# A Restormer block on one core: layer-norm statistics of two interleaved tiles per instruction, the TensorE convolution in two of three units of every band, and one common set of PSUM banks

## The chip, the cores and the metric

The kernel runs on one core of one Trainium2 chip. The metric is the device time of one execution in microseconds, given as the median of three runs. One execution was recorded by the hardware profiler; its page and its trace are what the prediction argues from. The engines are called by the names that the profile uses: PE (TensorE, matrix multiplication), PEld (its weight loads), DVE (VectorE), ACT (ScalarE), POOL (GpSimd) and SP (SyncE, which here only issues transfers).

## What is computed

The input is 16 images of 128 channels by 96 by 96 pixels in float32. For each image the reference computes a transformer block whose attention runs over channels, and then a feed-forward part with a depthwise convolution:

```
xn1 = layernorm(x over channels)
q, k, v = xn1 @ wq.T, xn1 @ wk.T, xn1 @ wv.T        # 8 heads of 16 channels
attn = softmax(l2norm(q) @ l2norm(k).T * scale)     # 16 x 16 per head, sums over all pixels
x = x + (attn @ v) @ wp.T
xn2 = layernorm(x over channels)
h1 = w_in @ xn2                                     # 128 -> 512 channels, 1x1
h2 = depthwise 3x3 of h1                            # 512 channels, zero padding
x = x + w_out @ gelu(h2)                            # 512 -> 128 channels, 1x1
```

## The kernel before, in words

Channels lie on the 128 partitions. An image is cut into 24 units of 4 rows (384 pixels, three tiles of 128 pixels) and 8 bands of 12 rows (three units each); the 512 hidden channels are four chunks of 128.

**Layer norms** (`norm_batch`, line 349). The norm runs over channels, which are partitions, so each tile is turned by PE into PSUM (`forth`, L374; pixels are now on partitions), DVE takes its statistics (`stats`, one `bn_stats` per tile, L380), five short DVE operations on 128x6 make mean and variance of the six tiles of a batch (`moments`, L389 to L393), POOL raises the variance to the power -0.5 (`power`, L397), one more short DVE operation makes the shift (`shift`, L401), ACT scales the tiles out of PSUM (`scaled`, L408), PE turns them back (`back`, L417), and ACT places them in the padded image `xn` (`place`, L432 for the second norm, L436 for the first). A `bn_stats` writes six numbers: count, mean and sum of squared deviations of the elements at even positions, and the same of those at odd positions; `moments` merges the two halves. The first norm (names with `a`) also adds each tile's product with itself to a 128x128 Gram matrix on PE (`gram`, L424), from which `attention` makes a single 128x128 matrix per image; the second norm (names with `b`) begins with `mix` (L364, that matrix times `xn`) and `residual` (L368, on DVE).

**Convolution.** For each band and each chunk, `conv_job` makes 14 rows of hidden values on PE in three matmuls of 490, 490 and 392 columns (`hidden`, L599), ACT copies each from PSUM into `h1` (`kept`, L606), and the nine taps of the depthwise filter are shared out. ACT multiplies tap 0 straight into `h3`, and taps 1 and 2 into buffers `pr` (L615). POOL issues a transfer that adds one `pr` to the other and a second that adds the sum to `h3` (`by_dma`, L626). The other six are DVE instructions on 128x1152 that each add to the same `h3` (`tap`, L623); these are called taps below. ACT then applies the gelu (L646). For chunk 3 of five of the eight bands (`PE_BANDS`, bands 1, 3, 5, 6 and 7) there is no such job: `by_matmuls` (L660) makes the convolved values of each unit by nine accumulating matmuls with a combined filter, and ACT takes the gelu out of PSUM (L668). `ffn_out` (L684) multiplies the four chunks by `w_out`, unit by unit; DVE adds the result to the image (L691), and SP stores the band.

**PSUM.** There are eight banks of 512 floats per partition: three for turned tiles (`p_tr`), one for tiles turned back (`p_b`), two shared by hidden rows, mixes and the PE convolution (`p_h`), one for the output (`p_o`), one for the Gram matrix (`p_g`).

**The order of the work.** `Plan` keeps a list of operations with an engine, a duration, a place (its priority, counted in convolution jobs) and the tiles that it reads and writes. `Plan.order` plays them through with these durations: an engine that falls idle takes the operation of lowest place among those that are ready and whose buffers are free. The order found is written out as the program, and each engine then runs its own part of it strictly in turn. An operation behind another of the same engine counts as ready when that one's duration is over; behind another engine's, after its `result` time, which is 430 to 550 ns longer for PE, DVE and ACT. Pools in `IN_TURN` give out their buffers in the order of the places. There are nine `h3` tiles (each one chunk of a band), three `h1` and three `pr`.

Of the kernel before, what the change touches and what calls it, by code (L numbers as in the profile page):

```python
# [20 lines left out]
PE_BANDS = (1, 3, 5, 6, 7)  # L21
DMA_TAPS = (1, 2)
BU = 2
# [3 lines left out]
IN_TURN = ("h3", "h1", "pr", "xb", "x1")  # L27
IN_ORDER = ("PE", "DVE", "ACT")
# [4 lines left out]
class Plan:  # L33
# [7 lines left out]
    def __init__(self, **pools):  # L41
        self.free = dict(pools)
        self.ops, self.writer, self.readers, self.users = [], {}, {}, {}

    def op(self, engine, ns, place, work, reads=(), writes=(), result=None):
# [21 lines left out]
        self.ops.append((engine, ns, place, work, list(needs), new, ns if result is None else result))  # L67

    def order(self):
# [27 lines left out]
        def room(k):  # L97
# [5 lines left out]
            for p, n in need.items():  # L103
                if free[p] < n:
# [3 lines left out]
        def dispatch(engine, time):  # L108
# [13 lines left out]
            for t in o[5]:  # L122
                free[t[0]] -= 1
# [16 lines left out]
        while events:  # L140
            time, _, kind, what = heapq.heappop(events)
            if kind != "look":
                for f in followers[what]:
                    if (ops[f][0] == ops[what][0] in IN_ORDER) == (kind == "idle"):
# [4 lines left out]
            if kind == "done":  # L149
                for t in held[what]:  # L150
                    pending[t] -= 1
                    if not pending[t]:
                        free[t[0]] += 1
                        wake(t[0], time)
                continue
# [11 lines left out]
def tile_restormer_block(  # L167
# [30 lines left out]
    TPU = UT // P  # L198
    NTOK = H * W
    HP, WP = H + 2, W + 2  # L200
    D = C // HEADS
    assert C == P and UT % P == 0 and H % BR == 0 and NCH == 4
# [22 lines left out]
    mhalf = const.tile([P, BU * TPU], F32, name="mhalf")  # L225
# [22 lines left out]
    with tc.tile_pool(name="setup", bufs=1) as sp, tc.tile_pool(name="setup2", bufs=2) as sp2:  # L248
# [10 lines left out]
        def transposed(dst, src):  # L259
            pt = p_tr.tile([P, P], F32, tag="tr", name="pt")  # L260
# [7 lines left out]
        pc = p_tr.tile([1, 2 * P], F32, tag="tr", name="pc")  # L268
# [36 lines left out]
    def x_unit(of, i, u):  # L305
# [5 lines left out]
        tr=3, b=1, h=2, o=1, g=1, batch=4, zT=3, x1=X1_BUFS, xb=XB_BUFS, h1=H1_BUFS, pr=PR_BUFS, h3=H3_BUFS  # L311
# [3 lines left out]
    def z_units(i, r0, r1):  # L315

        lo, hi = max(r0 - 1, 0) // UR, min(r1 - 2, H - 1) // UR
# [12 lines left out]
    def pe(ns, p, f, r, w):  # L330
        op("PE", ns, p, f, r, w, ns + 200 + SLACK)
# [439 lines left out]
```

## Time and profile before

| What | us |
|---|---|
| median of three runs (5211.49 to 5216.23) | 5215.31 |
| the profiled execution | 5207.15 |
| its span, first to last instruction | 5205.4 |
| PE busy | 4771.6 |
| DVE busy | 4736.2 |
| ACT busy | 4002.6 |
| POOL busy | 1592.3 |

A row of groups in the profile names a line of the kernel, an engine, the operation, what it writes and reads, the shapes and the count; behind the bar stand the busy time and the mean duration of one in ns, and behind the second bar the engine's idle time just ahead of them with what ended it. A row of the timeline has the start in us from the span's start, the time taken, the engine and the operation, merged where equal ones follow each other; the distance between the starts of two rows, where the engine has no idle time between, is what the first really costs its engine, since the end of one overlaps the start of the next. A float32 matmul stands as two MATMUL instructions, a transpose as one.

### The profile page before, as it was taken

What the parts mean: (1) busy time and instruction counts of PE and PEld (TensorE: products, weight loads), DVE (VectorE), ACT (ScalarE), POOL (GpSimd) and SP (SyncE); (2) the same over time, 40 slices, a digit from 0 to 9 for tenths busy, and PEclk for the clock granted to TensorE, in tenths of its full rate; (3) what the DMA queues carried; (4) which work ended last, traced back from release to release, by engine and by line L of the source; (5) the groups of instructions that cost most, each with busy time, mean ns of one, the idle gap of its engine ahead of it and who ended that gap; (6) DMA issues with size and microseconds to landing.
All of it is one profiled execution on the core that took longest, in us unless ns stands there. A gap on an engine that the chain in (4) does not pass through costs nothing.

```text
span 5205.4 us, 55115 instructions
## 1 busy us (share of the span) xinstructions
PE 4771.6 (92%) x18118; PEld 2835.9 (54%) x18118; DVE 4736.2 (91%) x8288; ACT 4002.6 (77%) x6768; POOL 1592.3 (31%) x1282
## 2 busy tenths in 40 slices
PE   6899999998989989999899999999899898998988
PEld 4455555555555555555555555555555555555544
DVE  3999999999999999999999999999999989989897
ACT  3877878778787787877878787787877878778675
POOL 1232323333233232333323233232332323233221
PEclk7999999999999999999999999999999999999999
DMA  2566666666676666666666666666766766666675
GB/s 88 116 146 148 146 137 155 146 141 158 129 157 138 147 155 130 151 141 148 153 141 150 137 151 148 144 140 137 158 146 137 158 133 151 137 141 148 129 150 124
DMA packets 182352, 740.52 MB, mean 142 GB/s; under 512 B 21168, under 2 KB 22192, under 8 KB 182064
## 3 DMA queue, kind: packets, MB, share of 16 engines
q0 software_dynamic: 124416, 509.66, 52.2%
q1 hardware_dynamic: 55296, 226.52, 12.5%
q8 instruction: 143, 2.34, 0.2%
q14 instruction: 145, 1.19, 0.1%
q10 hardware_dynamic: 2352, 0.81, 0.1%
HBM read 151.80 MB, written 75.50 MB: 44 GB/s over the span
## 4 chain that ended last, share of the span: by engine, by line
DVE 46%; PE 35%; ACT 8%; DMA 7%; issue 3%; POOL 2%; POOLq 0%; ACTq 0%
DVE h L623 33%; PE pc L660 15%; PE ph L599 7%; PE po L684 7%; DMA h<-pr 4%; DVE st_a L380 3%; DVE st_b L380 2%; ACT pr L615 2%; DMA pr<-pr 2%; DVE xTrue L368 2%; DVE xTrue L691 2%; PE pm L364 2%; PE g L424 2%; ACT h L615 1%; ACT zT_a L408 1%
## 5 line engine op out<-in xcount | busy, mean ns | idle before, releaser
L623 DVE SCALAR_TENSOR_TENSOR h<-h,dw,h 128x1152 f32<-128x1152 f32 x2592 | 3649.8, 1414 | 130.9 <-ACT h L615 90.5
L660 PE MATMUL pc<-xn,comp 128*128 128x384 f32 x4320 | 1580.8, 492 | 43.3 <-ACT h L606 23.4
L599 PE MATMUL ph<-xn,winT 128*128 128x490 f32 (+1 forms) x2592 | 1226.7, 566 | 136.8 <-ACT h L606 117.2
L684 PE MATMUL po<-h,woutT 128*128 128x384 f32 x3072 | 1171.7, 492 | 85.2 <-DVE xTrue L691 66.4
L660 PEld LDWEIGHTS pc<-xn,comp 128*128 128x128 f32 x4320 | 800.3, 192 | 622.5 <-issue 159.2
L615 ACT ACTIVATE pr<-h,dw 128x1152 f32<-128x1152 f32 x864 | 1067.4, 1258 | 68.4 <-DMA pr<-pr 67.3
L606 ACT COPY h<-ph 128x490 f32<-128x490 f32 x1296 | 697.8, 546 | 466.2 <-PE ph L599 456.1
L626 POOL DMA_DIRECT2D h<-pr x432 | 396.0, 917 | 1687.1 <-DVE h L623 455.6
L684 PEld LDWEIGHTS po<-h,woutT 128*128 128x128 f32 x3072 | 561.0, 190 | 513.3 <-DVE xTrue L691 127.6
L599 PEld LDWEIGHTS ph<-xn,winT 128*128 128x128 f32 x2592 | 455.6, 193 | 490.1 <-ACT h L606 234.2
L646 ACT ACTIVATE h<-h 128x1152 f32<-128x1152 f32 x432 | 507.1, 1174 | 255.1 <-DMA h<-pr 254.2
L397 POOL TENSOR_TENSOR rstd_b<-ve_b,mhalf 128x6 f32<-128x6 f32 x192 | 426.4, 2221 | 727.7 <-DVE ve_b L393 708.3
L626 POOL DMA_DIRECT2D pr<-pr x432 | 412.3, 954 | 655.8 <-ACT pr L615 604.1
L615 ACT ACTIVATE h<-h,dw 128x1152 f32<-128x1152 f32 x432 | 546.1, 1264 | 9.4
L397 POOL TENSOR_TENSOR rstd_a<-ve_a,mhalf 128x6 f32<-128x6 f32 x192 | 383.0, 1995 | 493.3 <-DVE ve_a L393 486.1
L408 ACT ACTIVATE zT_a<-pT_a,nb_a,rstd_a 128x128 f32<-128x128 f32 x1152 | 422.6, 463 | 101.4 <-DVE nb_a L401 91.9
L408 ACT ACTIVATE zT_b<-pT_b,nb_b,rstd_b 128x128 f32<-128x128 f32 x1152 | 428.2, 462 | 56.2 <-DVE nb_b L401 55.3
L691 DVE TENSOR_TENSOR xTrue<-po,xTrue 128x384 f32<-128x384 f32 x384 | 211.3, 550 | 132.2 <-PE po L684 131.8
L424 PE MATMUL g<-zT_a 128*128 128x128 f32 x2304 | 331.3, 287 | 0.0
L364 PE MATMUL pm<-xn,mwT 128*128 128x384 f32 x768 | 320.7, 501 | 3.6 <-ACT h L606 3.5
L380 DVE BATCH_NORM_STATS2 st_a<-pT_a 128x6 f32<-128x128 f32 x1152 | 260.0, 284 | 59.4 <-PE pT_a L374 59.2
L424 PEld LDWEIGHTS g<-zT_a 128*128 128x128 f32 x2304 | 310.5, 206 | 5.7 <-issue 0.6
(110 smaller groups left out, 3420.6 us busy)
## 6 DMA issues: line engine op xcount, KB each, us to landing
pr<-pr POOLq DMA_DIRECT2D x432, 576.0 KB, 6.1
h<-pr POOLq DMA_DIRECT2D x432, 576.0 KB, 5.0
xFalse<-in_x_dram SPq DMA_DIRECT2D x128, 576.0 KB, 4.7
xTrue<-in_x_dram SPq DMA_DIRECT2D x128, 576.0 KB, 4.8
out_dram<-xTrue SPq DMA_DIRECT2D x128, 576.0 KB, 5.0
win_sb<-in_L_conv_w_in_dram ACTq DMA_DIRECT2D x1, 256.0 KB, 10.9
wout_sb<-in_L_conv_w_out_dram ACTq DMA_DIRECT2D x1, 256.0 KB, 11.8
wv_sb<-in_L_conv_wv_dram ACTq DMA_DIRECT2D x1, 64.0 KB, 4.8
```

What stands on the lines that cost most here:

```text
L380: nc.vector.bn_stats(d["st"][:, (u - us[0]) * TPU + j, :], d["pT", u][:, j, :])
L397: nc.gpsimd.tensor_tensor(rstd, d["ve"], mhalf[:, :n], ALU.pow)
L408: nc.scalar.activation(zT[:, j, :], pT[:, j, :], AF.Identity, bias=d["nb"][:, c : c + 1], scale=d["rstd"][:, c : c + 1],)
L424: nc.tensor.matmul(grams[i][:, :P], lhsT=zT[:, j, :], rhs=zT[:, j, :], start=(u == 0 and j == 0), stop=(u == NU - 1 and j == TPU - 1),)
L599: nc.tensor.matmul(ph, lhsT=winT[:, n, :], rhs=xn[:, r0 + r : r0 + r + k, :], start=True, stop=True)
L606: nc.scalar.copy(d["h1"][:, r : r + min(5, BR + 2 - r), :], d.pop(("ph", r)))
L615: nc.scalar.activation(to, window(t), AF.Copy, scale=dw[:, n, t : t + 1])
L623: nc.vector.scalar_tensor_tensor(h3, window(t), dw[:, n, t : t + 1], h3, ALU.mult, ALU.add)
L626: nc.gpsimd.dma_start(out=to, in_=of, accum_op=ALU.add)
L646: act(t_act(BR * W), j + 1.5, lambda: nc.scalar.activation(h3s[g, n], h3s[g, n], AF.Gelu), [], h3)
L660: nc.tensor.matmul(d["pc"], lhsT=comp[:, t, :], rhs=xn[:, r0 + dy : r0 + dy + UR, dx : dx + W], start=(t == 0), stop=(t == 8),)
L684: nc.tensor.matmul(rows(d["po"]), lhsT=woutT[:, n, :], rhs=h3s[g, n][:, s * UR : (s + 1) * UR, :], start=(k == 0), stop=(k == NCH - 1),)
```

## The change

1. **Statistics.** A group is now four tiles (`QT = 4`) in one PSUM bank, independent of unit borders. `stats` reads two tiles at once with their elements alternating (`"p t c -> p c t"`), so that the even positions are one tile and the odd positions the other, and `bn_stats` gives the mean and the squared deviations of each: 1152 instructions of 256 elements for 2304 of 128. `moments` is gone; one short DVE operation (`variance`) and the shift remain for each group. The groups are 36 per image where there were 24 batches, and so are POOL's powers: 576 for 384.
2. **PE convolution.** `PE_UNITS = 2`: in every band, chunk 3 is made by matmuls in units 0 and 1 (256 units in all, 240 before), and in unit 2 by a small `conv_job` of 4 rows with two hidden matmuls of 294 columns, ACT for tap 0 and DVE for all eight other taps on 128x384; it uses no `pr` and no adding transfer. Full jobs are 384 (432 before).
3. **PSUM.** Turned tiles have two banks; hidden rows, mixes, tiles turned back, PE convolutions and outputs share five; the Gram matrix has one.
4. **The planner.** An operation has a time `own` after which followers on its own engine may start (130 ns more than its duration on DVE, 250 ns on ACT) besides its duration; in the meantime the engine may take something else. Every user of a buffer waits for the buffer's first user. `tr` has joined the pools that are given out in turn.

The diff, cut to its core:

```diff
-PE_BANDS = (1, 3, 5, 6, 7)
+PE_UNITS = 2
-BU = 2
+QT = 4
-IN_TURN = ("h3", "h1", "pr", "xb", "x1")
-IN_ORDER = ("PE", "DVE", "ACT")
+IN_TURN = ("tr", "h3", "h1", "pr", "xb", "x1")
...
                 self.users.setdefault(t, []).append(k)
+                needs[self.users[t][0]] = True
...
+            push(time + o[7], "own", k)
             push(time + o[1], "idle", k)
             push(time + o[6], "done", k)
...
-                    if (ops[f][0] == ops[what][0] in IN_ORDER) == (kind == "idle"):
+                    if (ops[f][0] == ops[what][0]) == (kind == "own"):
...
-    p_tr = ctx.enter_context(tc.tile_pool(name="p_tr", bufs=3, space=PSUM))
-    p_b = ctx.enter_context(tc.tile_pool(name="p_b", bufs=1, space=PSUM))
-    p_h = ctx.enter_context(tc.tile_pool(name="p_h", bufs=2, space=PSUM))
-    p_o = ctx.enter_context(tc.tile_pool(name="p_o", bufs=1, space=PSUM))
+    p_tr = ctx.enter_context(tc.tile_pool(name="p_tr", bufs=2, space=PSUM))
+    p_h = ctx.enter_context(tc.tile_pool(name="p_h", bufs=5, space=PSUM))
...
     def dve(ns, p, f, r, w):
-        op("DVE", ns, p, f, r, w, ns + 130 + SLACK)
+        op("DVE", ns, p, f, r, w, ns + 130 + SLACK, ns + 130)
...
-            for j in range(TPU):
-                nc.vector.bn_stats(d["st"][:, (u - us[0]) * TPU + j, :], d["pT", u][:, j, :])
...
+                nc.vector.bn_stats(
+                    d["st"][:, j, :], d["pT"][:, 2 * j : 2 * j + 2, :].rearrange("p t c -> p c t")
                 )
...
+            def variance():
+                d["mv"] = d["st"].rearrange("p j (t v) -> p (j t) v", v=3)
+                ve = d["ve"] = small.tile([P, QT], F32, tag="ve", name=f"ve_{name}_{q}")
+                nc.vector.tensor_scalar(ve, d["mv"][:, :, 2], 1.0 / C, EPS, ALU.mult, ALU.add)
...
+            def shift():
+                nb = d["nb"] = small.tile([P, QT], F32, tag="nb", name=f"nb_{name}_{q}")
+                nc.vector.scalar_tensor_tensor(nb, d["mv"][:, :, 1], -1.0, d["rstd"], ALU.mult, ALU.mult)
...
-    def conv_job(j, g, n):
+    def conv_job(j, g, n, s0, s1):
...
-        xn, r0 = xns[i % 2], b * BR
+        xn, r0, nr = xns[i % 2], b * BR + s0 * UR, (s1 - s0) * UR
...
+        taps = DMA_TAPS if nr == BR else ()
+        left = [t for t in range(1, 9) if t not in taps]
...
-        po = ("o", (g, s))
+        po = ("h", ("out", g, s))
...
+            s0 = PE_UNITS if n == PE_CHUNK else 0
+            if s0 < UPB:
+                jobs.append((j, g, n, s0, UPB))
+                j += (UPB - s0) / UPB
...
-                if composite(g):
-                    by_matmuls(start + 1 + s * (end - start) / UPB, g, s)
+                if s < PE_UNITS:
+                    by_matmuls(start + 0.5 + s * (end - start) / PE_UNITS, g, s)
```

The next two pieces are DVE's queue in the fourth image, before and then with the change. `h3_30_1` is the `h3` tile of band 30, chunk 1; `st`, `ve` and `nb` belong to the layer norms, and a `xTrue` written from `pm` or `po` is a residual or an output addition.

```order
L623 SCALAR_TENSOR_TENSOR h3_30_1_10113<-h1_30_1_10041,dw_104,h3_30_1_10113 128x1152 x3
L401 SCALAR_TENSOR_TENSOR nb_b4_0_10153<-m2_b4_0_10124,rstd_b4_0_10135 128x6
L623 SCALAR_TENSOR_TENSOR h3_30_1_10113<-h1_30_1_10041,dw_104,h3_30_1_10113 128x1152 x3
L691 TENSOR_TENSOR xTrue_3_5_8442<-po_29_0_10106,xTrue_3_5_8442 128x384
L623 SCALAR_TENSOR_TENSOR h3_30_2_10190<-h1_30_2_10142,dw_104,h3_30_2_10190 128x1152 x3
L368 SCALAR_TENSOR_TENSOR xTrue_4_0_9543<-pm_4_2_10209,d_4_9988,xTrue_4_0_9543 128x384
L623 SCALAR_TENSOR_TENSOR h3_30_2_10190<-h1_30_2_10142,dw_104,h3_30_2_10190 128x1152 x2
L380 BN_STATS st_b4_1_10232<-pT_b4_1_2_10223 128x6 x3
```

Here is DVE's queue with the change, in bands 28 and 27 of the same image.

```order
L406 SCALAR_TENSOR_TENSOR nb_a4_13_8950<-st_a4_13_8898,rstd_a4_13_8933 128x4
L398 TENSOR_SCALAR ve_b3_13_8952<-st_b3_13_8928 128x4
L370 SCALAR_TENSOR_TENSOR xTrue_3_6_8329<-pm_3_19_8941,d_3_7317,xTrue_3_6_8329 128x384
L638 SCALAR_TENSOR_TENSOR h3_28_1_8857<-h1_28_1_8840,dw_98,h3_28_1_8857 128x1152
L638 SCALAR_TENSOR_TENSOR h3_28_2_8947<-h1_28_2_8935,dw_98,h3_28_2_8947 128x1152
L406 SCALAR_TENSOR_TENSOR nb_b3_13_8981<-st_b3_13_8928,rstd_b3_13_8956 128x4
L712 TENSOR_TENSOR xTrue_3_3_7506<-po_27_0_8945,xTrue_3_3_7506 128x384
L638 SCALAR_TENSOR_TENSOR h3_28_1_8857<-h1_28_1_8840,dw_98,h3_28_1_8857 128x1152
L391 BN_STATS st_a4_14_8999<-pT_a4_14_8985 128x6
L638 SCALAR_TENSOR_TENSOR h3_28_2_8947<-h1_28_2_8935,dw_98,h3_28_2_8947 128x1152
```

Before, two or three taps on one tile follow each other, and each needs the sum that the one ahead of it has written; now something else stands between almost any two of them. Counted over the whole queue, a tap of 1152 elements directly behind a tap on its own tile occurs 1113 times before and 132 times now; among the 1024 new taps of 384 elements it occurs 249 times.

The next piece is PE's queue in band 40, which is band 0 of the sixth image and had all of its chunk 3 on DVE before.

```order
L599 MATMUL ph_40_2_10_12897<-xn1_216,winT_109 128x392
L684 MATMUL po_39_0_12867<-h3_39_2_12703,woutT_110 128x384
L599 MATMUL ph_40_3_0_12906<-xn1_216,winT_109 128x490
L599 MATMUL ph_40_3_5_12920<-xn1_216,winT_109 128x490
L684 MATMUL po_39_1_12930<-h3_39_3_12694,woutT_110 128x384
```

With the change the same band reads so on PE:

```order
L683 MATMUL pc_40_0_12111<-xn1_210,comp_105 128x384 x8
L385 MATMUL pT_b5_4_12140<-ident_73,xTrue_5_1_11440 128x128 x2
L385 MATMUL pT_b5_4_12140<-ident_73,xTrue_5_2_11735 128x128 x2
L445 MATMUL pB_b5_4_12145<-ident_73,zT_b5_3_12130 128x128 x3
L385 MATMUL pT_a6_0_12149<-ident_73,xFalse_6_0_11323 128x128 x4
L683 MATMUL pc_40_0_12111<-xn1_210,comp_105 128x384
L616 MATMUL ph_40_2_0_12161<-xn1_210,winT_103 128x490
```

The band has 18 convolution matmuls (`pc_40_0` and `pc_40_1`) that it did not have; they stand between the hidden rows of its other chunks. The gelu that frees the bank of `pc_40_0` stands on ACT behind the first product of the small job, since that is the first user of the shared `h3` tile:

```order
L623 COPY h1_40_3_12216<-ph_40_3_3_12205 128x294
L634 ACTIVATE h3_40_3_12254<-h1_40_3_12216,dw_98 128x384
L453 ACTIVATE xn0_209,sums_6_12262<-pB_a6_0_12249 128x4x96
L689 ACTIVATE h3_40_3_12254<-pc_40_0_12111 128x384
L647 ACTIVATE h3_40_0_12074<-h3_40_0_12074 128x1152
```

On PE the two matmuls for `ph_40_3` come 14 rows behind the start of `pc_40_0`, so this bank stays taken over that stretch.

More of the change, by code (lines that the diff above doesn't have):

```diff
@@ L41, in __init__, with op @@
     def __init__(self, **pools):
-        self.free = dict(pools)
+        self.free = {p: list(range(n)) for p, n in pools.items()}
+        self.slot = {}
         self.ops, self.writer, self.readers, self.users = [], {}, {}, {}
-    def op(self, engine, ns, place, work, reads=(), writes=(), result=None):
+    def op(self, engine, ns, place, work, reads, writes, result, own=None):
         k = len(self.ops)
@@ L142, in order @@
             if kind != "look":
[L143 to L144 removed]
+                for f in followers[what] if kind != "idle" else ():
+                    if (ops[f][0] == ops[what][0]) == (kind == "own"):
                         left[f] -= 1
@@ new lines, in channels, with back, place @@
+        def channels(s, u):
+            d = {}
+            def back():
+                d["pB"] = p_h.tile([P, UT], F32, tag="h", name=f"pB_{name}_{u}")
+                for j in range(TPU):
+                    q, k = divmod(u * TPU + j, QT)
+                    nc.tensor.transpose(d["pB"][:, j * P : (j + 1) * P], zTs[q][:, k, :], ident)
+            def place():
+                if second:
+                    nc.scalar.activation(interior(i, u), rows(d["pB"]), AF.Identity, bias=b2, scale=w2)
+                    return
```

287 lines of the change are left out of this document (134 added, 153 removed).

## The prediction

> **What bounds the kernel now.** I read the page first, then a table of stretches, then the waits of DVE and PE, then the timelines of both where they run without a gap. The page calls PE the busiest engine, with DVE close behind:
>
> ```profile
> PE 4771.6 (92%) x18118; PEld 2835.9 (54%) x18118; DVE 4736.2 (91%) x8288; ACT 4002.6 (77%) x6768; POOL 1592.3 (31%) x1282
> ```
>
> Which of the two sets the time is seen in 40 us stretches of one image. After the length stand the busy times of PE, PEld, DVE, ACT and POOL. The last two rows are the start of the run, called the head here, and its long middle; what follows 5180 is the tail.
>
> ```profile
> 1960.00:2000.00 40.00, 40.00 (x143) 23.71 (x142) 36.24 (x57) 32.56 (x51) 10.92 (x9) 1.00 0.63 134
> 2000.00:2040.00 40.00, 40.00 (x133) 23.18 (x132) 36.45 (x52) 25.48 (x39) 9.96 (x8) 1.00 0.58 124
> ...
> 2120.00:2160.00 40.00, 37.83 (x156) 22.95 (x154) 36.59 (x71) 34.88 (x63) 11.76 (x10) 1.00 0.65 148
> 2160.00:2200.00 40.00, 35.36 (x153) 21.73 (x154) 39.54 (x69) 33.00 (x64) 13.34 (x11) 1.00 0.75 160
> ...
> 0.00:160.00 160.00, 104.24 (x496) 78.90 (x496) 64.73 (x297) 67.71 (x187) 29.63 (x39) 0.82 0.24 73
> 160.00:5180.00 5020.00, 4648.98 (x17569) 2747.25 (x17570) 4667.21 (x7986) 3933.27 (x6580) 1561.82 (x1242) 0.98 0.67 145
> ```
>
> The bound changes within the image. From 1960 to 2040 (the last three bands, all with PE convolution) PE has no gap and DVE idles 7 us of 80. From 2160 DVE is full (39.54 of 40) and PE idles. From 2120, where bands of both kinds mix, both lose 2 to 3.5 us of 40. Over the middle of 5020 us DVE idles 5020 - 4667 = 353 us. The waits say for whom:
>
> ```profile
> DVE xTrue L691 <- PE po L684: 131.8, 83, 7.8
> DVE h L623 <- ACT h L615: 90.5, 76, 2.6
> DVE st_a L380 <- PE pT_a L374: 59.2, 34, 3.7
> DVE st_b L380 <- PE pT_b L374: 39.0, 37, 2.8
> DVE xTrue L368 <- PE pm L364: 35.9, 26, 4.8
> PE ph L599 <- ACT h L606: 117.2, 95, 3.7
> PE po L684 <- DVE xTrue L691: 66.4, 71, 1.7
> ```
>
> DVE waits 131.8 + 59.2 + 39.0 + 35.9 = 266 us for PE. PE in turn waits 117 + 66 = 184 us for a PSUM bank that ACT or DVE still reads: hidden rows have two banks, outputs one.
>
> **What the parts cost.** Durations overlap, so I price by the distance between starts. First DVE:
>
> ```profile
> 2006.72 0.68 DVE L380 BATCH_NORM_STATS2 st_b<-pT_b 128x6 f32<-128x128 f32 x3
> 2007.44 0.17 DVE L389 TENSOR_TENSOR dm_b<-st_b 128x6 f32<-128x6 f32 x1
> ...
> 2007.61 0.17 DVE L391 TENSOR_TENSOR m_b<-st_b 128x6 f32<-128x6 f32 x1
> 2007.69 0.16 DVE L392 SCALAR_TENSOR_TENSOR dm_b<-dm_b 128x6 f32<-128x6 f32 x1
> 2007.88 0.17 DVE L393 SCALAR_TENSOR_TENSOR ve_b<-q_b,dm_b 128x6 f32<-128x6 f32 x1
> 2007.96 4.32 DVE L623 SCALAR_TENSOR_TENSOR h<-h,dw,h 128x1152 f32<-128x1152 f32 x3
> 2012.20 0.16 DVE L401 SCALAR_TENSOR_TENSOR nb_b<-m_b,rstd_b 128x6 f32<-128x6 f32 x1
> 2012.32 4.33 DVE L623 SCALAR_TENSOR_TENSOR h<-h,dw,h 128x1152 f32<-128x1152 f32 x3
> ...
> 2028.52 1.41 DVE L623 SCALAR_TENSOR_TENSOR h<-h,dw,h 128x1152 f32<-128x1152 f32 x1
> 2029.84 0.61 DVE L368 SCALAR_TENSOR_TENSOR xTrue<-pm,d,xTrue 128x384 f32<-128x384 f32 x1
> 2030.37 0.68 DVE L380 BATCH_NORM_STATS2 st_b<-pT_b 128x6 f32<-128x128 f32 x3
> 2030.97 0.54 DVE L691 TENSOR_TENSOR xTrue<-po,xTrue 128x384 f32<-128x384 f32 x1
> 2031.43 1.41 DVE L623 SCALAR_TENSOR_TENSOR h<-h,dw,h 128x1152 f32<-128x1152 f32 x1
> 2032.76 0.68 DVE L380 BATCH_NORM_STATS2 st_b<-pT_b 128x6 f32<-128x128 f32 x3
> ```
>
> A tap costs 1.33 us where something independent follows (2031.43 to 2032.76), and (4.33 - 1.41) / 2 = 1.46 where the next tap needs its result: 0.13 more. *Taps before:* 2592 x 1.33 + 1113 dependent pairs x 0.13 = 3592 us. *Full taps after:* 2304 x 1.33 + 132 x 0.13 = 3081, so **-511**.
>
> *Small taps, new:* 1024 of 384 elements. No row has one. The nearest is L368, the same operation on 384 elements out of PSUM, 0.53 (2029.84 to 2030.37); the lower end is a third of a full tap, 0.44. I take 0.50, nearer the row of the same size: 512 + 249 dependent pairs x 0.13 = **+544**, ends 483 and 575. [...]
>
> *Statistics:* three cost 0.60 (2030.37 to 2030.97), so 0.20 each, and 0.12 more when L389 follows at once (2006.72 to 2007.44), which happens 348 times: 2304 x 0.20 + 348 x 0.12 = 503 us. The difference between a full tap and L368, 0.80 us for 768 elements, is 1.04 ns an element, so 256 elements cost 0.20 + 128 x 0.00104 = 0.333. After: 1152 x 0.333 + 33 x 0.12 = 388, **-115**. That holds if the alternating read runs at full rate; the other end, two steps an element, is 0.60 and +188 instead. The only rows with spaced reads are in `moments`: L391 reads every sixth element and takes 0.08, as the unspaced L393 does. Six elements prove little, but that is the row, so I take the full rate.
>
> *Short operations:* 384 x (0.52 from 2007.44 to 2007.96, and 0.12 for the shift) = 246 us. After: 576 x (0.12 + 0.12) = 138, with the full 0.12 for both because each now stands between taps: **-108**.
>
> Residuals and additions stay. DVE: -511 + 544 - 115 - 108 = **-190 us**.
>
> Now PE:
>
> ```profile
> 2003.46 0.82 PE L599 MATMUL ph<-xn,winT 128*128 128x392 f32 x2
> 2004.12 2.10 PE L684 MATMUL po<-h,woutT 128*128 128x384 f32 x6
> 2006.05 0.49 PE L374 MATMUL pT_b<-ident,xTrue 128*128 128x128 f32 x3
> 2006.38 0.81 PE L660 MATMUL pc<-xn,comp 128*128 128x384 f32 x2
> 2007.03 0.98 PE L599 MATMUL ph<-xn,winT 128*128 128x490 f32 x2
> 2007.85 2.10 PE L660 MATMUL pc<-xn,comp 128*128 128x384 f32 x6
> 2009.78 0.81 PE L684 MATMUL po<-h,woutT 128*128 128x384 f32 x2
> ```
>
> Three matmuls of 384 columns cost 1.93, so 0.643 each; 490 columns 0.82, 392 columns 0.66, a transpose 0.11. Convolutions go from 2160 to 2304 matmuls: +93 us. Hidden rows go from 432 x (2 x 0.82 + 0.66) = 994 to 384 x 2.30 + 256 x 0.495 (294 columns, by length) = 1010: +16. PE: **+109 us**. By these distances PE needs 1389 (convolution) + 994 + 988 (1536 outputs) + 247 (384 mixes) + 507 (4608 transposes) + 253 (1152 Gram products at two transposes' cost) = 4378 us before, and 4487 after. DVE needs 4736 - 190 = 4546. So both fit into the old span with room, and neither has a light band left: every band holds 18 convolution matmuls on PE and 18 full and 8 small taps on DVE.
>
> ACT loses 144 of its 1296 products on 128x1152 and 48 of 432 gelus, and gains as many elements in small pieces, less those that DVE now takes; nothing is added here, since at 77% busy ACT has room for either sign. Of the 864 adding transfers 96 go. POOL gets 192 more powers and 96 fewer issues:
>
> ```profile
> L397 POOL TENSOR_TENSOR rstd_b<-ve_b,mhalf 128x6 f32<-128x6 f32 x192 | 426.4, 2221 | 727.7 <-DVE ve_b L393 708.3
> POOL h L626 <- DVE h L623: 455.6, 87, 9.3
> ```
>
> The powers add up to 192 x 2.22 = 426 us there, under its 69% idle. If that cover is gone it is in the queue: a power behind an issue that waits for a tap is late by 455.6 / 87 = 5.2 us, its group keeps one of two banks of turned tiles, and PE's next forward transpose, with all PE work behind it, waits. SP's loads and stores keep their number. The change adds two waits: a forward transpose needs the residuals of up to two units, and the gelu of `pc_0` waits for the small job's first product.
>
> **The sum.** The middle's DVE work is 4667 - 190 = 4477 us. Its idle time is my choice: 255 if half of PE's 184 us of bank waits go and DVE's waits with them, roughly one for one; 416 if the whole run is like the mixed stretch from 2120, where DVE is 36.59 / 40 = 91.5% busy (4477 / 0.915 - 4477). Five shared banks speak for the first, PE without slack for the second. I take 305, a little nearer the first. The head is a chain (turn, statistics, power, scale) in which no engine is full: PE is busy 104 of 160 us. It gets 18 groups of four on two banks for 12 batches of six on three; I leave it at 160 and allow 20 either way. With the tail as now: 160 + 4477 + 305 + 25 (5180 to 5205.4) = 4967 us of span. The profiled execution took 5207.15 for 5205.4, and the median 5215.31 is 8 above it, so the forecast is 4967 + 2 + 8 = **4977 us**.
>
> **The rivals.** That the change does what it says is plain from the program: the 1152 statistics, 256 PE units and 384 full jobs all stand in its queues.
>
> *Two full engines hold each other up* (0.20). For: in the mixed stretch both lose. Against: two-bank and one-bank pools cause much of it. Idle is 416: 160 + 4477 + 416 + 25 + 10 = 5088 us.
>
> *The alternating read goes at half rate* (0.10). Each `bn_stats` takes 0.60, DVE has 1152 x 0.267 = 308 us more, 4785 in the middle, and is the only bound. At its best here, 39.54 / 40, that makes 4785 / 0.988 + 195 = 5038; at today's 93% (4667 / 5020) 5340; between them some 5190, so a gain, nothing or a loss. For it: no row reads PSUM spaced. Against: L391. [...]
>
> *PE is blocked on a bank* (0.08), the slower side. The bank of `pc_0` stays taken over 14 PE rows and until ACT has copied and multiplied the small job's rows; with an output held too, three banks serve hidden rows, mixes and turned tiles, and a blocked matmul stops all of PE. The gain of 238 us is 1.86 us a band, so it decides from there; one more wait per band like today's longest for ACT (3.7) makes 4977 + 128 x 3.7 = 5451 us. Against: the planner counts these banks.
>
> **Chances.** Forecast 0.62. A measurement of this kernel tells about 0.2% (10 us) from no change. Faster: 0.62 + 0.20 + 0.04 of the half-rate case = 0.86. Same: 0.03 of it and 0.01 of the blocked case = 0.04. Slower: 0.03 + 0.07 = 0.10. The range reaches from idle 255 with small taps two thirds of the way to their low end (4977 - 50 - 41 = 4886, taken as 4885) to idle 416 with small taps at their high end (5088 + 31 = 5119, taken as 5125). It leaves out most of the half-rate and blocked cases and the edges of the forecast, some 0.2.
>
> **What would show it.** Right: DVE and PE even over an image, both at 94% or more; a 384-element tap near 0.50, `bn_stats` near 0.33; PE's waits on ACT and DVE for banks below 100 us. Wrong: `bn_stats` at 0.45 or more; PE waits at hidden rows or forward transposes above today's; DVE idle above 416 us.

## The result and the profile after

The changed kernel takes 4796.1 us in the median of four runs (4795.38 to 4798.47); beside it the kernel before takes 5213.4 us (four runs, 5210.29 to 5216.23). The ratio is 0.92, with a 95% interval of 0.9185 to 0.9216. The forecast of 4977 us had the direction and missed the size by 181 us; the time lies below the range too.

The line of engines of the profile after:

```profile
PE 4659.3 (97%) x18630; PEld 2925.7 (61%) x18630; DVE 4580.8 (96%) x6720; ACT 3923.1 (82%) x6960; POOL 1594.1 (33%) x1378
```

Both engines are now nearly full. DVE's busy time fell by 155 us (4736.2 to 4580.8), while the span fell by 411 (5205.4 to 4794.1). So 256 us of the gain are idle time of DVE that is gone: 469 us before (5205.4 - 4736.2), 213 now. Not all of that was waiting for another engine: the waits of DVE that the profile lists with what ended them add up to 395 us before and 190 now, so 204 us of the 256 are such waits; the rest, 75 us before and 23 now, lies nearly all in gaps too short to be listed. The stretches of one image, with the same columns as before, and then the middle and the head:

```profile
1960.00:2000.00 40.00, 39.72 (x171) 25.74 (x170) 39.02 (x57) 34.21 (x67) 14.23 (x13) 1.00 0.60 134
2000.00:2040.00 40.00, 39.86 (x167) 25.69 (x166) 39.89 (x61) 33.87 (x64) 17.24 (x15) 1.00 0.78 174
2040.00:2080.00 40.00, 37.06 (x162) 23.83 (x160) 34.62 (x53) 31.95 (x64) 14.93 (x12) 1.00 0.58 130
...
2120.00:2160.00 40.00, 39.72 (x137) 23.15 (x136) 39.97 (x52) 31.93 (x50) 11.26 (x11) 1.00 0.71 148
2160.00:2200.00 40.00, 38.34 (x144) 23.36 (x143) 40.00 (x56) 31.50 (x52) 14.19 (x13) 1.00 0.68 144
...
160.00:4769.00 4609.00, 4532.86 (x18029) 2836.89 (x18028) 4484.58 (x6494) 3832.88 (x6749) 1552.09 (x1322) 1.00 0.66 145
0.00:160.00 160.00, 110.84 (x563) 80.44 (x564) 80.30 (x208) 84.67 (x206) 39.41 (x53) 0.93 0.33 90
```

Where PE was the full one before (up to 2040) and DVE (from 2160), both are now within 2 us of 40. DVE loses more in one place of the image, 5.4 us from 2040 to 2080. In the middle DVE idles 4609 - 4484.6 = 124 us, where it idled 353. The waits that carried the argument before, as they are now, DVE's first and then PE's:

```profile
DVE h L638 <- ACT h L634: 51.6, 38, 3.8
DVE st_a L391 <- PE pT_a L385: 26.1, 20, 4.5
DVE xTrue L712 <- PE po L705: 23.3, 40, 4.8
...
DVE xTrue L370 <- PE pm L366: 10.6, 22, 1.3
DVE st_b L391 <- PE pT_b L385: 10.2, 10, 4.3
PE pB_b L445 <- ACT h L623: 23.1, 16, 2.6
PE pc L683 <- ACT h L623: 14.8, 14, 1.7
...
PE ph L616 <- ACT h L623: 1.9, 3, 1.4
```

DVE's four waits for PE, 266 us before, are 26.1 + 23.3 + 10.6 + 10.2 = 70. PE's wait of 117.2 us at the hidden rows is 1.9; that of 66.4 us at the outputs no longer stands among PE's waits. DVE's waits for POOL's powers rose, from 9 to 31 us. The chain of work that ended last, by engine, first in the kernel before:

```profile
DVE 46%; PE 35%; ACT 8%; DMA 7%; issue 3%; POOL 2%; POOLq 0%; ACTq 0%
```

and then in the kernel after:

```profile
DVE 53%; PE 32%; DMA 7%; ACT 6%; issue 2%; POOL 1%; ACTq 0%; POOLq 0%; DVEq 0%
```

It runs through DVE more and through ACT and PE less, in a shorter span.

### The profile page after: what moved, and what is told of

Read it like the earlier page. It is cut to its first block, busy times and chain, and to the rows that moved or that the text cites. A ratio compares the mean times of both kernels' runs of the same rounds, so it can differ in the third digit from the quotient of the medians.

```text
span 4794.1 us, 54774 instructions
## 1 busy us (share of the span) xinstructions
PE 4659.3 (97%) x18630; PEld 2925.7 (61%) x18630; DVE 4580.8 (96%) x6720; ACT 3923.1 (82%) x6960; POOL 1594.1 (33%) x1378
## 4 chain that ended last, share of the span: by engine, by line
DVE 53%; PE 32%; DMA 7%; ACT 6%; issue 2%; POOL 1%; ACTq 0%; POOLq 0%; DVEq 0%
DVE h L638 43%; PE pc L683 10%; PE po L705 7%; PE ph L616 6%; DMA pr<-pr 4%; DVE xTrue L370 3%; DVE st_b L391 2%; DMA h<-pr 2%; PE g L421 2%; DVE xTrue L712 2%; DVE st_a L391 2%; PE pm L366 2%; ACT pr L634 1%; ACT zT_a L411 1%; PE pB_a L445 1%
## 5 line engine op out<-in xcount | busy, mean ns | idle before, releaser
L638 DVE SCALAR_TENSOR_TENSOR h<-h,dw,h 128x1152 f32<-128x1152 f32 (+1 forms) x3328 | 3789.2, 1164 | 65.2 <-ACT h L634 51.6
L616 PE MATMUL ph<-xn,winT 128*128 128x490 f32 (+2 forms) x2816 | 1147.8, 523 | 9.0 <-ACT xn L453 6.0
L634 ACT ACTIVATE pr<-h,dw 128x1152 f32<-128x1152 f32 x768 | 957.5, 1264 | 74.2 <-DMA pr<-pr 74.1
L623 ACT COPY h<-ph 128x490 f32<-128x490 f32 (+2 forms) x1408 | 703.7, 530 | 213.6 <-PE ph L616 187.5
L647 ACT ACTIVATE h<-h 128x1152 f32<-128x1152 f32 (+1 forms) x512 | 517.5, 1014 | 152.5 <-DMA h<-pr 94.7
L402 POOL TENSOR_TENSOR rstd_b<-ve_b,mhalf 128x4 f32<-128x4 f32 x288 | 471.7, 1638 | 500.6 <-DVE ve_b L398 497.2
L402 POOL TENSOR_TENSOR rstd_a<-ve_a,mhalf 128x4 f32<-128x4 f32 x288 | 468.1, 1626 | 326.0 <-DVE ve_a L398 296.3
L634 ACT ACTIVATE h<-h,dw 128x1152 f32<-128x1152 f32 (+1 forms) x512 | 565.3, 1104 | 11.3
L449 ACT ACTIVATE xn<-pB_b,b,w 128x384 f32<-128x384 f32 x384 | 258.1, 692 | 30.2 <-PE pB_b L445 29.0
L391 DVE BATCH_NORM_STATS2 st_a<-pT_a 128x6 f32<-128x256 f32 x576 | 240.9, 422 | 26.3 <-PE pT_a L385 26.1
```

The source lines that it names most:

```text
L391: nc.vector.bn_stats(d["st"][:, j, :], d["pT"][:, 2 * j : 2 * j + 2, :].rearrange("p t c -> p c t"))
L402: nc.gpsimd.tensor_tensor(rstd, d["ve"], mhalf, ALU.pow)
L616: nc.tensor.matmul(ph, lhsT=winT[:, n, :], rhs=xn[:, r0 + r : r0 + r + k, :], start=True, stop=True)
L623: nc.scalar.copy(d["h1"][:, r : r + min(step, nr + 2 - r), :], d.pop(("ph", r)))
L634: nc.scalar.activation(to, window(t), AF.Copy, scale=dw[:, n, t : t + 1])
L638: nc.vector.scalar_tensor_tensor(h3, window(t), dw[:, n, t : t + 1], h3, ALU.mult, ALU.add)
```

## The experiments

What had to be found was where DVE's 256 us of idle time went. Three theories: A, the even split of the convolution took it (every band now gives PE and DVE the same mix); B, the common PSUM banks took it; C, the planner's new rule took it, by which a follower on the same engine comes later and something else stands between. Whether the statistics' price was read rightly was tried beside these. All kernels are the one after with pieces of it undone or altered. DVE idle is the span less DVE's busy time.

| Kernel | median us | ratio to before, 95% | span | PE busy | DVE busy | DVE idle |
|---|---|---|---|---|---|---|
| before | 5213.4 | 1 | 5205.4 | 4771.6 | 4736.2 | 469 |
| after | 4796.1 | 0.9185 to 0.9216 | 4794.1 | 4659.3 | 4580.8 | 213 |
| e1 split undone | 4847.0 | 0.9284 to 0.9315 | 4847.3 | 4618.4 | 4442.5 | 405 |
| e2 banks undone | 4960.2 | 0.9503 to 0.9535 | 4959.1 | 4726.0 | 4608.6 | 350 |
| e3 rule undone | 4972.6 | 0.9530 to 0.9558 | 4971.2 | 4713.2 | 4749.3 | 222 |
| e4 statistics undone | 4979.5 | 0.9544 to 0.9572 | 4979.8 | 4732.4 | 4833.0 | 147 |
| e5 all four undone | 5260.2 | 1.0076 to 1.0106 | 5255.5 | 4784.6 | 4849.7 | 406 |
| e6 statistics alone | 5231.6 | 1.0023 to 1.0049 | 5223.8 | 4773.3 | 4575.1 | 649 |
| e7 banks alone | 5073.5 | 0.9721 to 0.9750 | 5073.3 | 4702.9 | 4824.8 | 249 |
| e8 rule alone | 5186.1 | 0.9928 to 0.9961 | 5185.5 | 4765.6 | 4744.4 | 441 |
| e9 split alone | 5569.4 | 1.0667 to 1.0699 | 5567.8 | 4966.8 | 5054.9 | 513 |
| e10 gelu earlier | 4774.3 | 0.9142 to 0.9172 | 4764.7 | 4648.0 | 4571.9 | 193 |
| e11 small products | 5422.7 | 1.0388 to 1.0423 | 5416.7 | 4863.6 | 4549.7 | 867 |
| e12 both of these | 5434.4 | 1.0406 to 1.0445 | 5429.8 | 4898.3 | 4585.3 | 845 |

### One part undone

**e1, the even split.** Chunk 3 is again made by PE in whole bands 1, 3, 5, 6 and 7, with places counted as before.

```diff
-PE_UNITS = 2
+PE_BANDS = (1, 3, 5, 6, 7)
...
-            s0 = PE_UNITS if n == PE_CHUNK else 0
+            s0 = UPB if n == PE_CHUNK and g % NB in PE_BANDS else 0
...
-                if s < PE_UNITS:
-                    by_matmuls(start + 0.5 + s * (end - start) / PE_UNITS, g, s)
+                if g % NB in PE_BANDS:
+                    by_matmuls(start + 1 + s * (end - start) / UPB, g, s)
```

> The changed kernel with the old share of the PE convolution: bands 1, 3, 5, 6 and 7 of each image make all three units of chunk 3 on PE, the other bands none (240 units instead of 256, 432 full jobs, no small ones). By the prices of the profile DVE has 2592 taps at 1.33 for 2304 at 1.33 and 1024 at 0.53, some 160 us less, and PE 109 us less. Theory A (the even split is what took DVE's idle time away): idle goes back from 213 us to above 400, so the time rises in spite of the smaller work, to 4900 or more. Theory B (the shared banks did it) and theory C (the planner's order did it): idle stays near 213, and the time is 4800 or less.

Measured: 4847.0 us, 51 slower than after. It stands between the bounds given, so none of the three theories is the whole. DVE has 138 us less work (the uneven split needs no small taps) and 192 us more idle time. The even split does take idle time, and pays most of it back in small taps.

**e2, the common banks.** Turned tiles two banks, hidden rows three, tiles turned back, outputs and the Gram matrix one each.

```diff
+    p_b = ctx.enter_context(tc.tile_pool(name="p_b", bufs=1, space=PSUM))
-    p_h = ctx.enter_context(tc.tile_pool(name="p_h", bufs=5, space=PSUM))
+    p_h = ctx.enter_context(tc.tile_pool(name="p_h", bufs=3, space=PSUM))
+    p_o = ctx.enter_context(tc.tile_pool(name="p_o", bufs=1, space=PSUM))
...
```

> The changed kernel with separate banks: two for turned tiles, three for hidden rows, mixes and PE convolutions, one for tiles turned back, one for outputs, one for the Gram matrix. The work of every engine is the same. Theory B (shared banks): PE's waits on ACT and DVE for banks go back to 150 us or more and the time rises by 120 us or more, to 4920. Theories A and C: the rise is below 50 us.

Measured: 4960.2 us, 164 slower: B holds. DVE's work is nearly the same (+28), its idle time 137 us more. The waits of DVE and PE in this kernel:

```profile
DVE h L640 <- ACT h L636: 127.7, 88, 6.4
DVE xTrue L372 <- PE pm L368: 45.7, 39, 3.1
DVE xTrue L714 <- PE po L707: 41.0, 33, 5.6
...
PE pc L685 <- ACT h L625: 45.9, 45, 3.4
PE ph L618 <- DVE xTrue L372: 40.7, 32, 2.2
```

PE waits for banks again at the hidden rows and the convolution, and DVE waits for PE's mixes and outputs and for ACT's products; ACT's copies, from which the products are made, wait 407 us for PE's hidden rows, where they wait 188 in the kernel after.

**e3, the planner's rule.** A follower on the same engine counts as ready at the end of the duration again.

```diff
-        op("DVE", ns, p, f, r, w, ns + 130 + SLACK, ns + 130)
+        op("DVE", ns, p, f, r, w, ns + 130 + SLACK, ns)
...
-        op("ACT", ns, p, f, r, w, ns + 250 + SLACK, ns + 250)
+        op("ACT", ns, p, f, r, w, ns + 250 + SLACK, ns)
```

> The changed kernel with a follower on the same engine ready when the duration is over (no added 130 or 250 ns in the planner), so that taps on one tile follow each other directly again. About 900 to 1000 more dependent pairs at 0.13 us make 120 to 130 us more on DVE. Theory C (the order): that and more idle, 4950 or more. Theories A and B: the 120 to 130 us and no more, 4900 to 4930; less if PE sets the time.

Measured: 4972.6 us, 176 slower; the idle time is 222 against 213. What comes back is in the main DVE work, 168 us of it. The idle time hides two changes that nearly cancel: the gaps too short to be listed grow from 23 to 83 us, and the listed waits fall from 190 to 139, those for PE from 84 to 48. DVE's timeline in this kernel:

```profile
2010.47 1.27 DVE L638 SCALAR_TENSOR_TENSOR h<-h,dw,h 128x384 f32<-128x384 f32 x2
2011.66 0.55 DVE L712 TENSOR_TENSOR xTrue<-po,xTrue 128x384 f32<-128x384 f32 x1
...
2019.35 2.86 DVE L638 SCALAR_TENSOR_TENSOR h<-h,dw,h 128x1152 f32<-128x1152 f32 x2
2022.12 0.15 DVE L406 SCALAR_TENSOR_TENSOR nb_b<-st_b,rstd_b 128x4 f32<-128x4 f32 x1
...
2026.83 0.76 DVE L391 BATCH_NORM_STATS2 st_a<-pT_a 128x6 f32<-128x256 f32 x2
2027.62 0.17 DVE L398 TENSOR_SCALAR ve_a<-st_a 128x4 f32<-128x4 f32 x1
```

Two small taps in a row on one tile take 1.19 us (2010.47 to 2011.66) for 2 x 0.53, two full ones 2.77 for 2 x 1.33, two statistics with their variance right behind 0.79 for 2 x 0.34: 0.11 to 0.13 us for each dependent pair. In DVE's queue the dependent pairs are 890 full and 663 small taps against 132 and 249 after, and 567 variances behind their statistics against 33: 758 x 0.11 + 414 x 0.13 + 534 x 0.11 = 196 us. A part of each pair is such a gap: a tap of 1152 elements lasts 1.42 us, and the dependent one starts 1.45 us behind its start. So the 196 us are to be set against 168 us more work and 60 us more gaps, 228 in all; they explain the larger part. Of the 256 us of idle time that went, the 52 us of short gaps are therefore put down in the main to C; the longer waits are not.

**e4, the statistics.** One `bn_stats` for each tile of 128 elements, five short operations to merge the halves, everything else as after.

```diff
-                nc.vector.bn_stats(
-                    d["st"][:, j, :], d["pT"][:, 2 * j : 2 * j + 2, :].rearrange("p t c -> p c t")
-                )
+                for k in range(2 * j, 2 * j + 2):
+                    nc.vector.bn_stats(d["st"][:, k, :], d["pT"][:, k, :])
...
-                nc.vector.tensor_scalar(ve, d["mv"][:, :, 2], 1.0 / C, EPS, ALU.mult, ALU.add)
+                nc.vector.tensor_tensor(dm, st[:, :, 1], st[:, :, 4], ALU.subtract)
+                nc.vector.scalar_tensor_tensor(ve, st[:, :, 2], C * EPS, st[:, :, 5], ALU.add, ALU.add)
+                nc.vector.tensor_tensor(nb, st[:, :, 1], st[:, :, 4], ALU.add)
+                nc.vector.scalar_tensor_tensor(dm, dm, 0.25, dm, ALU.mult, ALU.mult)
+                nc.vector.scalar_tensor_tensor(ve, ve, 1.0 / C, dm, ALU.mult, ALU.add)
```

> The changed kernel with one statistics instruction per tile and the five short operations that merge the halves, in groups of four: 2304 x 0.20 for 1152 x 0.34 is 69 us more, and 576 x 0.40 for four more short operations 230 us: 300 us more on DVE. If DVE sets the time in the changed kernel (96% busy) all of it shows: 5050 to 5100. If PE (97% busy) sets it as much, some 100 us vanish in DVE's idle time: 4950 to 5000.

Measured: 4979.5 us, 183 slower, with 252 us more DVE work and 66 less idle. The time lies in the second of the two ranges: about seven tenths of the work show, the rest went into DVE's idle time. At 97% busy DVE is the fuller engine of this kernel, where PE has 95%.

The four losses add up to 51 + 164 + 176 + 183 = 574 us, more than the whole gain of 417. So the parts are not independent, and the next kernels ask which needs which.

### One part alone

e5 undoes all four with the edits of e1 to e4, its banks as before (three for turned tiles, one, two, one, one); groups of four tiles, their 576 powers, turned tiles given out in turn and the rule of the first user stay. e6 to e9 each leave one part in. If the parts were independent (theory 1) each would gain alone what it lost when undone; if they depend on each other (theory 2) it would not.

> The changed kernel with all four parts undone: old split of the PE convolution, old statistics, separate banks (3, 1, 2, 1, 1), old ready rule. It differs from the kernel before in its groups of four tiles instead of batches of six (576 groups of short operations for 384: 192 x 0.64 = 123 us more on DVE), in turned tiles being given out in turn and in the wait for a buffer's first user. DVE should be busy 4736 + 123 = 4859 us; with the idle time of before, 469 us, the time is 5330. If the groups or the first-user rule alone changed the idle time, it is off from that by more than 60.

> All undone but the statistics, which are those of the change: 252 us less DVE work than with all undone. Theory 1 (each part is worth by itself what undoing it cost): 183 us below the run with all undone. Theory 2 (DVE's savings only show in the stretches in which DVE is the full engine, about two thirds of an image, as long as the split is uneven and the banks are separate): 170 us or less, with DVE's idle time higher by 80 or more.

> All undone but the banks: two for turned tiles, five shared. DVE's work stays. Theory 1: 164 us below the run with all undone. Theory 2: the banks help most where both engines are near full, which is rare with the uneven split: below 100 us.

> All undone but the ready rule of the planner: a follower on the same engine is ready 130 ns (DVE) or 250 ns (ACT) after the duration. Some 168 us less on DVE. Theory 1: 176 us below the run with all undone. Theory 2: 110 us or less.

e5 takes 5260.2 us. The DVE work came as computed (4850), the idle time was 406 and not 469: with the old parts and smaller groups the kernel is 47 us slower than before. The time is off by 70 from the 5330 expected, so the groups, the turn of the turned tiles or the rule of the first user took idle time themselves; which of them did is not tested. Against e5, the statistics alone gain 29 us (183 when undone from the full change), the banks alone 187 (164), the rule alone 74 (176). Theory 2 holds for the statistics and the rule; it missed for the banks, which stand by themselves: alone they take 157 us of DVE's idle time (406 to 249) at nearly the same work, and undone they bring back 137 (e2). No run has exactly two of the parts, so which pair makes the statistics pay is not seen. The line of engines of e6 and its largest waits:

```profile
PE 4773.3 (91%) x18118; PEld 2874.1 (55%) x18118; DVE 4575.1 (88%) x5984; ACT 3995.7 (76%) x6768; POOL 1725.6 (33%) x1474
...
DVE h L640 <- ACT h L636: 182.4, 165, 4.3
DVE xTrue L714 <- PE po L707: 168.3, 115, 7.8
...
PE ph L618 <- ACT h L625: 112.2, 109, 5.0
```

DVE has 275 us less to do than in e5, as little as in the kernel after, and idles 243 us longer. It waits for PE's outputs and ACT's products, while PE still waits 112 us for a bank at the hidden rows. So the statistics are worth 29 us beside the old split, banks and rule, and 183 beside the new ones. That the banks make the difference is likely from these waits and not shown. In e7, where the banks are common, PE's wait for ACT's copies at the hidden rows is down to 9 us from 136 in e5, but another wait for a bank, at the tiles turned back, now heads PE's list:

```profile
PE pB_b L450 <- ACT h L628: 105.7, 79, 3.9
```

DVE's waits for PE fell all the same, from 181 us in e5 to 82.

> All undone but the even split of the PE convolution. DVE has some 140 us more work than with all undone (1024 small taps at 0.53 for 288 full ones at 1.33), PE 109 us more. If the even split takes idle time away by itself (192 us less of it was seen when the split alone was undone), the time is 50 us below the run with all undone, 5210. If it needs the shared banks (three PE convolution matmul groups no longer come in a row, but a bank of the two for hidden rows is held longer), DVE's idle time does not fall and the time is 5350 or more.

e9 takes 5569.4 us, 309 more than e5 and 356 more than before: the split alone does harm. Its line of engines and its waits:

```profile
PE 4966.8 (89%) x18630; PEld 2916.2 (52%) x18630; DVE 5054.9 (91%) x10176; ACT 3968.6 (71%) x6960; POOL 1591.9 (29%) x1378
...
PE ph L623 <- ACT h L630: 149.3, 247, 1.9
PE po L712 <- DVE xTrue L719: 133.3, 101, 2.4
PE pm L368 <- ACT h L630: 77.1, 85, 1.9
...
DVE xTrue L372 <- PE pm L368: 208.8, 117, 4.8
```

Under the old rule 880 of the 1024 small taps stand right behind one on their own tile: 1024 x 0.53 + 880 x 0.13 = 657 us in place of 288 full taps (288 x 1.33 = 383) and 442 dependent pairs of full taps (442 x 0.11 = 49), some 225 us more DVE work by these prices, and 205 measured. Two hidden-row banks now serve PE convolutions in every band, and PE waits 149 us there and 133 at the outputs. Of the four parts this one depends most on the others: 309 us of loss alone, 51 of gain in the full change.

### Two ways further

**e10, the PE units planned ahead of the small job.** Only the order in which the planner is told of them changes, so that the gelu of `pc_0` is the first user of the shared `h3` tile and needn't wait for the small job's product.

```diff
+        for g in range(NB * i, NB * (i + 1)):
+            start, end = first[g], first[g + 1]
+            for s in range(PE_UNITS):
+                by_matmuls(start + 0.5 + s * (end - start) / PE_UNITS, g, s)
         for job in jobs:
...
-                if s < PE_UNITS:
-                    by_matmuls(start + 0.5 + s * (end - start) / PE_UNITS, g, s)
```

> The changed kernel with the PE units registered ahead of the small job, so that the gelu of pc_0 is the first user of the h3 tile and frees its bank before the small job's first product. If the long hold of that bank costs anything (the prediction's slower rival), the time falls by 20 us or more. If the five banks have room for it, it stays within 10 us of the changed kernel.

Measured: 4774.3 us (4766.45 to 4778.13), 22 less than after, and the fastest of all kernels here. All its runs lie below all of after's. Holding that bank, with whatever else this order moves, costs 22 us in 128 bands, 0.17 us a band, a twentieth of the rival's price. What fell most on DVE is its wait for ACT's products, from 51.6 to 20.9 us, so it is not shown that the bank is the whole reason.

**e11, products by ACT and adding transfers in the small jobs too,** so that DVE has six small taps a band in place of eight; e12 is this with e10's edit.

```diff
-        taps = DMA_TAPS if nr == BR else ()
+        taps = DMA_TAPS
```

> The changed kernel with taps 1 and 2 of the small jobs made as products on ACT and added by transfers, as in the full jobs: 256 taps of 0.53 us leave DVE (136 us less), ACT gets 100 us more, POOL 256 more issues. If DVE sets the time in the changed kernel, 80 to 130 us less: 4670 to 4715. If PE sets it as much (97% busy, some 4490 us by the distances of its starts), less than 50 us.

> Both edits of the two runs ahead together: the sum of their gains if each comes from another engine, no more than the larger one if they do not.

Measured: 5422.7 and 5434.4 us, slower by 627 and 660 than after and e10, where a small gain or none was expected. DVE does 31 us less in e11, where 136 were expected, and idles 867 us. Among its waits, by engine:

```profile
DVE xTrue L712 <- PE po L705: 254.4, 191, 20.0
...
PE po L705 <- ACT h L647: 120.3, 52, 9.2
...
ACT pr L634 <- DMA h<-pr: 215.3, 97, 6.0
...
POOL h L643 <- DMA pr<-pr: 414.0, 145, 7.9
```

ACT waits for a free `pr`, POOL holds its queue for a landing, the gelus come late, PE waits for them at the outputs and DVE for PE. The small jobs have joined the queue for the three `pr` buffers: 128 more jobs with two transfers of 192 KB each, 3.0 us from issue to landing. That the buffers in turn are the cause is read from these waits; more buffers were not tried.

## Why the prediction was right or wrong

**The step that failed is the idle time of the middle: "305", chosen between 255 and 416.** The span was forecast as 160 + 4477 + 305 + 25; measured it is 160 + 4484.6 + 124.4 + 25.1. The DVE work of the middle is off by 8 us and the idle time by 181, the whole error. The lower end of the choice was wrong as well. It let half of PE's 184 us of bank waits go (353 less 92 is 261, a little above the 255); at those two places nearly all went, and PE's waits for ACT and DVE together fell from 410 us to 119.5. Nor did the even split stand in that bound at all: undone by itself it brings back 192 us of idle time (e1), the banks 137 (e2). Together that is more than the 256 us that went, so the two overlap; and the split takes idle time only beside the other parts: alone it adds 107 (e9 against e5). The other bound took the mixed stretch from 2120 as a sample of what two full engines lose to each other, though that stretch ran on the two-bank and one-bank pools that the change removes.

A smaller step failed beside it. The 0.13 us of a dependent pair was priced as DVE work, but in the profile 0.035 of it is a gap that counts as idle time (in the kernel before, such a pair of taps has starts 1.45 us apart and the first lasts 1.42). So with 981 pairs fewer some 34 us were taken off the work that should have come off the idle time, where the sum had no term for them.

**DVE's work** came out at -155 us where -190 was forecast. That the middle was met within 8 us is partly luck: its work fell by 183 us, but the head does 16 us more than before and the tail 12 more (4.3 to 15.9), which the sum did not provide for. Counted over the whole trace, each operation until it ends or the next one starts:

| | before | after | change | forecast |
|---|---|---|---|---|
| full taps | 3552.9 | 3070.2 | -482.7 | -511 |
| small taps | | 564.6 | +564.6 | +544 |
| statistics | 493.8 | 395.6 | -98.2 | -115 |
| short operations | 226.9 | 93.1 | -133.8 | -108 |

The rest is 5 us less. Taps and statistics after were priced well (3070 for 3081, 396 for 388); the short operations were put too high on both sides (246 and 138 for 227 and 93). The taps before were put 39 us too high: 3552.9 - 2592 x 1.33 leaves 106 us for 1113 dependent pairs, 0.095 each and not 0.13, since the gaps, 1113 x 0.035 = 39 us, are not in this count. DVE's timeline after has the new prices:

```profile
2010.20 0.43 DVE L391 BATCH_NORM_STATS2 st_a<-pT_a 128x6 f32<-128x256 f32 x1
2010.54 1.40 DVE L638 SCALAR_TENSOR_TENSOR h<-h,dw,h 128x1152 f32<-128x1152 f32 x1
2011.86 0.16 DVE L398 TENSOR_SCALAR ve_a<-st_a 128x4 f32<-128x4 f32 x1
...
2018.57 0.61 DVE L638 SCALAR_TENSOR_TENSOR h<-h,dw,h 128x384 f32<-128x384 f32 x1
2019.10 0.61 DVE L370 SCALAR_TENSOR_TENSOR xTrue<-pm,d,xTrue 128x384 f32<-128x384 f32 x1
```

A small tap takes 0.53 us, as the row of the same size had it; the 0.50 gave a third of a full tap too much weight. A full tap takes 1.32 and a `bn_stats` of two tiles 0.34.

**The alternating read** runs at full rate: 0.34 us where 0.333 was forecast and 0.60 was the rival's price. The small row of six elements (0.08 us, spaced as unspaced) had told it rightly, though, as the prediction says, it proves little.

**Two full engines hold each other up** is refuted: PE at 97% and DVE at 96% share the span. **PE blocked on the bank of `pc_0`** is small if it is there: e10, which frees the bank earlier, gains 22 us and not 128 x 3.7.

**PE's +109 us** cannot be read from its busy time, which fell by 112 although PE has 512 instructions more. The stretches at half clock (below) account for up to some 90 us of that; the rest may be matmuls that ran alone, an estimate: a pair of 392 columns lasts 0.82 us and its successor starts 0.66 us behind its start, so a pair without a successor counts 0.16 more. How many there are was not counted. **POOL** was expected to gain 192 powers at 2.22 us; its busy time stayed (1592.3 to 1594.1). A power of four columns is shorter than one of six (1.64 us for 2.22), so the 576 powers take 940 us where the 384 took 809; the 96 adding transfers fewer save 71 us of issuing, and the rest is overlap (the groups add up to 1654 us before and 1710 after, 62 and 116 above POOL's busy time):

```profile
L402 POOL TENSOR_TENSOR rstd_b<-ve_b,mhalf 128x4 f32<-128x4 f32 x288 | 471.7, 1638 | 500.6 <-DVE ve_b L398 497.2
```

**The head** was left at 160 us. In the same 160 us DVE now does 80.3 us of work where it did 64.7, so by DVE's work 16 us were won there, inside the 20 allowed.

Of the signs that were named, evenness above 94%, `bn_stats` near 0.33 and short bank waits all came. The bank waits came more fully than the number that was built beside them.

## What to carry to other kernels

When two engines are both above 90% busy and each waits for the other through small pools, price the pools first: here a cut of 275 us in one engine's work gave 29 us with the old banks, split and rule, one of 252 us gave 183 beside the new ones, and the common banks gave 187 us by themselves. An idle time that is sampled from a stretch of the old kernel carries the old kernel's pools with it, so the lower end for a change that removes them should let all of their waits go, not half. A pause behind a dependent instruction is partly idle time in a profile (0.035 of 0.13 us for the taps here): price it from start to start, and take it off the same account it stands on. Undo parts one by one and also put them in one by one: where the two disagree, the parts depend on each other, and a part that does harm alone (the even split, +309 us) can still belong to the best version.

## What was not expected of the hardware

The granted clock of PE rose from 0.978 over the span to 0.995, and no term of the prediction stood for that. Before, (1 - 0.978) x 5205 = 115 us of full-speed clock were withheld, after 24. All the withheld clock in the middle lies in pieces of 3.41 us or a multiple of it at half speed (0.50 or 0.51 in each). Three neighbouring pieces of the kernel before, the columns as in the other stretches:

```profile
2098.39:2101.80 3.41, 1.19 (x4) 0.33 (x3) 3.34 (x3) 2.74 (x4) 1.05 (x2) 0.99 0.58 114
2101.80:2105.21 3.41, 3.41 (x15) 3.08 (x16) 0.82 (x3) 2.98 (x9) 0.73 (x1) 0.51 1.02 195
2105.21:2108.62 3.41, 3.41 (x19) 2.26 (x18) 3.34 (x10) 2.42 (x5) 2.24 (x1) 1.00 0.24 48
```

PE is busy 1.19 us in the first, runs at 0.51 of its clock in the second, and DVE, which idled 0.07 us in the first, idles 2.6 us in the second. The sums over the 39 slow pieces of the middle, first with every piece shifted to 3.41 us earlier (the seven pieces that are longer than 3.41 us then lie partly over themselves):

```profile
sum 160.46, PE 79.88 PEld 41.50 DVE 155.85 ACT 133.95 POOL 77.11; mean PE 2.05 PEld 1.06 DVE 4.00 ACT 3.43 POOL 1.98
```

then the slow pieces themselves:

```profile
sum 160.41, PE 151.58 PEld 93.50 DVE 141.97 ACT 104.99 POOL 55.85; mean PE 3.89 PEld 2.40 DVE 3.64 ACT 2.69 POOL 1.43
```

and every piece shifted 3.41 us back, past the slow ones:

```profile
sum 160.35, PE 158.68 PEld 99.43 DVE 141.40 ACT 113.68 POOL 43.42; mean PE 4.07 PEld 2.55 DVE 3.63 ACT 2.91 POOL 1.11
```

In the mean PE is half idle, then slow, and DVE, which idles 4.6 us in the first, idles 18.4 and 19.0 in the two that follow, where its share of the whole middle (353 of 5020) would be 11.3 each: some 15 us of DVE's idle time before, an estimate by this count, or 8 if the 6.7 us that DVE idles below its share in the first are set against it. So a pause of PE seems to be paid a second time, in the clock. The pause need not be a wait for a bank: in the first of the three pieces PE waits 1.64 us for a gelu and 0.58 for scaled tiles. In the stretches ahead of the slow pieces PE was busy half the time in the mean (79.88 of 160.46 us; those of one piece's length from 0 to 3.26 of 3.42), so how long a pause it takes is not shown. The clock goes with the split more than with the banks: 0.984 with the split alone (e9) against 0.967 without (e5), 0.983 with the split undone (e1) against 0.995, and 0.973 with the banks alone (e7). How much of the gain is the clock's, apart from the pauses that lower it, no run separates: e7 is 140 us faster than before at a lower clock.
